# Gated experts with a four-sequence product scheme: the order of the closing pairs, and where their X and the down forms are made

## The chip, the cores and the metric

One core of a Trainium2 chip. The metric is the device time of the whole program in microseconds, the median over runs.

## The reference

A residual block of gated experts. For each of 8 sequences x[b] (512 x 256), with 8 experts and one shared expert of width 1024:

```python
g = jnp.einsum('bsd,edf->ebsf', h, Wg)
u = jnp.einsum('bsd,edf->ebsf', h, Wu)
expert_outs = jnp.einsum('ebsf,efd->ebsd', jax.nn.silu(g) * u, Wd)
expert_output = jnp.einsum('be,ebsd->bsd', gating_probs, expert_outs)
shared = jnp.einsum('bsf,fd->bsd', jax.nn.silu(h @ Sg) * (h @ Su), Sd)
return (1.0 - sg) * expert_output + sg * shared        # and x is added
```

All is float32.

## The kernel before, in words

**Units.** The work is cut into 36 units: two halves (four sequences each), nine experts (the shared one is the ninth), two groups of four 128-row blocks of the width. A unit takes four blocks of gate and up weights against four sequences, 16 products each, and builds them from fewer matmuls by sums and differences over six pairs of indices, `PAIRS`. Units are numbered from 0; units 0 to 17 are the first half, 18 to 35 the second. `u.opens` marks units 0 and 18. `closes(u)` marks the unit whose down products finish the accumulators of its half: unit 17, and unit 34, since unit 35, the last one, does its down products in another way (`tail`).

**Gate and up.** `gate_up(u, nxt)` is a generator of 52 steps ("G"): 16 steps of the hub (`Q_step`, `P_step`, `R1_step`), then six for each pair p (`R1_step`, L536, for the next pair, and `R_step`, L546). After the four `R_step` of pair p = (i, j) both `h_[i, j]` and `h_[j, i]` exist, the second one later; `finish` makes them (SiLU on ScalarE, L476, then L481 on VectorE). L541 and L551 are VectorE's work on the PSUM banks of these products. Then `h_sums` makes the tile X of the pair, the difference of the two h (L562), and notes four sums for later: rows and cols. `add_sum` does one of these sums on GpSimd (L573). A unit has 24 of them; some 14 are done while its pairs run, one at every second step, and about ten are left over for the first steps of the unit behind.

**Down.** `down(u, acc)` is a second generator ("D") for the same unit. It starts at step `TAKE` = 22 of its own unit and runs on through the first 22 steps of the unit behind. A fixed string orders both: `HUB` is "GGD" eight times, `BLOCK` is "GGDGGDGGD" for a pair. So three matmul products go by between one D step and the next. For a pair, `pair(p)` has three D steps:
- r: `Wd[p][i]` times `h_[i, j]` into a PSUM bank A that is then held (L635). It is added to the accumulator B of j (L599).
- S: `Wd[p][j]` times `h_[j, i]`. For pairs 0 to 3 (`OWN`), in most units, ScalarE first copies the accumulator S into the bank (L611), PE adds to it (L612), and ScalarE copies it back (`carried`). In a closing unit there is no copy back: the bank is subtracted from the accumulators B of i and V of p (L601). For pairs 4 and 5 the product s goes to a fresh bank (L635) with the same two subtractions.
- `Ud[p]` times X, added into A (L658). In a closing unit VectorE then adds the accumulator V to A (L662), and puts A onto the two accumulators b (L599, L601 or L603, by the factor 1/d).

There are two banks for down, po0 and po1; `new_po` takes them in turn and passes over a held one. After the pairs come the products p and q of the sums: `cols` in q (L635, or L612 in some units), `rows` in p (L612, named b), mixed with pair 5 in the order 0, 1, 2, 3, 4, p0, q0, 5, q1, p1, q2, p2, q3, p3.

**Down forms.** `make_ad` (four sums of 128x128, L407 to L411, and a doubling, L449) and `d_forms` (L456, L461) prepare the down weights of a unit on GpSimd, in its hub.

**Order.** PE and POOL run in the order in which the program is written down (`manual_schedule`); the order of VectorE and ScalarE is made by a planner. Tile `X` has two buffers, `ud` and `wd` six.

Of the kernel before, what the change touches and what calls it, by code (L numbers as in the profile page):

```python
# [12 lines left out]
ALU = mybir.AluOpType  # L13
# [4 lines left out]
def kernel(  # L18
# [38 lines left out]
    B, S, D = x.shape  # L57
    E, _, F = Wg.shape
# [5 lines left out]
    NH = B // NI  # L64
    CI = (0.0, 1.0, -1.0, 2.0)
    PAIRS = ((1, 0), (0, 2), (3, 0), (1, 2), (3, 1), (3, 2))

    OWN = (0, 1, 2, 3)

    const = ctx.enter_context(tc.tile_pool(name="const", bufs=1))  # L70
    wpool = ctx.enter_context(tc.tile_pool(name="w", bufs=5))
# [24 lines left out]
    gp = nc.gpsimd  # L96
    ve = nc.vector
# [206 lines left out]
    def first_order(u, made, *what):  # L304

        if u.n == 0:
            u.issued[what] = made
            for late, early in BEHIND.items():
                if what in (late, early) and late in u.issued and early in u.issued:
                    issue_after(u.issued[late], u.issued[early])  # L310
# [55 lines left out]
    units = []  # L366
# [84 lines left out]
    def d_forms(u, p):  # L451

        i, j = PAIRS[p]
        lo, hi = min(i, j), max(i, j)
        U = upool.tile([P, P], F32, tag="ud", name=f"ud{u.name}_{p}", bufs=6)
        gp.tensor_tensor(U, u.ad[i], u.ad[j], ALU.subtract)  # L456
        W = upool.tile([P, 2, P], F32, tag="wd", name=f"wd{u.name}_{p}", bufs=6)
        at, d = U.unsqueeze(1).to_broadcast([P, 2, P]), CI[i] - CI[j]
        for c, a in ((2.0, u.a2), (1.0, u.raw_d)):
            if d >= c:  # L460
                gp.tensor_tensor(W, at, a[:, lo : hi + 1 : hi - lo, 0:P], ALU.subtract)  # L461
                at, d = W, d - c
        u.Ud[p] = U
        u.Wd[p] = {lo: W[:, 0], hi: W[:, 1]}
# [90 lines left out]
    def h_sums(u, p):  # L555


        i, j = PAIRS[p]
        if u.n + 1 == len(units):
            return  # L560
        u.X[p] = tpool.tile([P, S], F32, tag="t", name=f"X{p}_{u.name}")
        first_order(u, ve.tensor_sub(u.X[p], u.h_[j, i], u.h_[i, j]), "X", p)  # L562
        for k, l in ((i, j), (j, i)):
            for which, n in (("rows", k), ("cols", l)):
                u.sums.append((which, n, (k, l)))
# [13 lines left out]
    def closes(u):  # L579

        return u.n + (2 if u.h + 1 == NH else 1) == len(units) * (u.h + 1) // NH

    def down(u, acc):

        def tile_of(key):
            acc[key] = apool.tile(
                [P, S], F32, tag=f"acc{key[0]}{key[1]}", name=f"acc{key[0]}{key[1]}_{u.h}"
            )
            return acc[key]

        def put(key, bank, s):

            if key not in acc:
                if s == 1.0:
                    nc.scalar.copy(tile_of(key), bank)
                else:
                    nc.scalar.mul(tile_of(key), bank, s)
            elif s == 1.0:
                ve.tensor_add(acc[key], bank, acc[key])  # L599
            elif s == -1.0:  # L600
                ve.tensor_sub(acc[key], acc[key], bank)  # L601
            else:
                ve.scalar_tensor_tensor(acc[key], bank, s, acc[key], ALU.mult, ALU.add)  # L603

        def seeded(key, w, b):

            po, k = new_po(f"{key[0]}{key[1]}_{u.name}")
            full = key in acc and not turned[k]
            turned[k] = False
            if full:  # L610
                nc.scalar.copy(po, acc[key])  # L611
            nc.tensor.matmul(  # L612
                po, w, b, start=not full, stop=True, skip_group_check=full
            )
            return po, full

        def carried(key, w, b):
            po, full = seeded(key, w, b)
            if full:
                nc.scalar.copy(acc[key], po)  # L620
            else:
                put(key, po, 1.0)
            return po if full else acc[key]

        def carried_with(key, w, b, half, s):
            po, full = seeded(key, w, b)
            assert full
            ve.scalar_tensor_tensor(
                acc[key], xhub[u.h, key[1]][:, half], s, po, ALU.mult, ALU.add
            )  # L630

        def single(key, w, b):
            po, k = new_po(f"{key[0]}{key[1]}_{u.name}")
            turned[k] = False
            nc.tensor.matmul(po, w, b, start=True, stop=True)  # L635
            return po, k

        def pair(p):
            i, j = PAIRS[p]
            d = CI[i] - CI[j]  # L640
            A, k = single(("r", p), u.Wd[p][i], u.h_[i, j])
            put(("B", j), A, 1.0)
            held[k] = True
            yield
            args = u.Wd[p][j], u.h_[j, i]
            if p in OWN and not closes(u):
                carried(("S", p), *args)
            else:
                if p in OWN:
                    o, full = seeded(("S", p), *args)  # L650
                    if not full:
                        ve.tensor_add(o, o, acc["S", p])
                else:
                    o, _ = single(("s", p), *args)
                put(("B", i), o, -1.0)
                put(("V", p), o, -1.0)
            yield
            nc.tensor.matmul(  # L658
                A, u.Ud[p], u.X[p], start=False, stop=True, skip_group_check=True
            )  # L660
            if closes(u):
                ve.tensor_add(A, A, acc["V", p])  # L662
                put(("b", i), A, 1.0 / d)
                put(("b", j), A, -1.0 / d)
            else:
                put(("V", p), A, 1.0)
            held[k] = False
            po_next[0] = 1 - k
            yield

        done = {}
        for what in (0, 1, 2, 3, 4, "p0", "q0", 5, "q1", "p1", "q2", "p2", "q3", "p3"):
            if isinstance(what, int):
                yield from pair(what)
                continue
            i = int(what[1])
            extra = carry_on.get(u.n)
            if extra is not None and extra[0] == what:
                flush_sums(u, "rows" if what[0] == "p" else "cols", i)
                if what[0] == "p":  # L680
                    key, w, b = ("b", i), u.raw_d[:, i, 0:P], u.rows[i]
                else:
                    key, w, b = ("B", i), u.ad[i], u.cols[i]
                carried_with(key, w, b, *extra[1:])
            elif what[0] == "p":
                flush_sums(u, "rows", i)
                done[what] = carried(("b", i), u.raw_d[:, i, 0:P], u.rows[i])
            else:
                flush_sums(u, "cols", i)
                po, _ = single(("q", i), u.ad[i], u.cols[i])  # L690
                put(("B", i), po, 1.0)
                done[what] = po
            if closes(u) and f"p{i}" in done and f"q{i}" in done:
                if CI[i] != 0.0:
                    put(("B", i), done[f"p{i}"], -CI[i])
                for r in (0, 1):
                    ends[u.h, i, r] = acc["bB"[r], i]
            yield
# [75 lines left out]
    def gate_up(u, nxt):  # L774
# [19 lines left out]
        for kind, i, m in hub_steps(u):  # L794
            if (kind, i, m) == ("P", 3, 0) and u.n or (kind, i, m) == ("Q", 1, 0) and u.n == 0:
                seed(u, 0)
            if (kind, i, m) == ("P", 3, 0) and u.n == 0:
                seed(u, 1)
            if kind == "Q":
                Q_step(u, i, m)  # L800
                if u.n == 0 and (i, m) == (3, 1):
                    for p, make in ahead[3:]:
                        make(u, p)
            elif kind == "P":
                P_step(u, i, m)
                if u.n == 0 and m == 1 and i in (1, 3):
                    for p, make in ahead[:2] if i == 1 else ahead[2:3]:
                        make(u, p)
            else:
                R1_step(u, 0, m)  # L810
            step += 1
            if step == 2 and u.n and nxt is not None:
                make_ad(u)
            if step in (3, 5, 7, 9, 11, 13) and u.n and nxt is not None:
                d_forms(u, (step - 3) // 2)
            yield
        if u.n == 0:
            make_ad(u)
# [58 lines left out]
                carry_on[3 + len(carry_on)] = f"{what}{i}", half, s  # L877

    TAKE = 22


    ends = {}
# [27 lines left out]
    for u in units:  # L910
# [6 lines left out]
        for what in FIRST if u.n == 0 else LAST if nxt is None else ORDER:  # L917
            if what == "G":
# [12 lines left out]
                    nc.sync.dma_start(*outgoing.pop(0))  # L931
                if nG > TAKE and nG % 2 == 0 and u.sums:
                    add_sum(u)
                for _ in range(2 if u.n and units[u.n - 1].opens else 1):
                    if nG < TAKE and u.n and units[u.n - 1].sums:
                        add_sum(units[u.n - 1])
                next(g)
# [63 lines left out]
```

## Time and profile before

| | us |
|---|---|
| median of 3 runs | 2439.89 (2439.74 to 2440.24) |
| profiled execution | 2439.38 |
| its span | 2437.6 |
| PE busy | 2427.2 |
| POOL busy | 2077.4 |
| DVE busy | 1926.9 |
| ACT busy | 1239.3 |

The span runs from the first to the last instruction of the program on the core; the execution's own time has 1.78 us around it. PE is TensorE's matmul queue, POOL is GpSimd, DVE is VectorE, ACT is ScalarE. Busy times of an engine are added without overlap. In answers by window the columns are PE, PEld (weight load), DVE, ACT, POOL with the number of instructions in brackets, then the granted TensorE clock, the DMA share and GB/s. A line of waits reads: who waited, for whom, us in total, times, longest. A product of 128x512 in float32 is two PE instructions in the profile.

### The profile page before, as it was taken

The page shows a single profiled execution, that of the slowest core. Times are in us where ns is not written, and L with a number is a line of the kernel's source. Part 1 is how long each engine was busy: PE and PEld are TensorE (multiplying, and loading weights), DVE is VectorE, ACT ScalarE, POOL GpSimd, SP SyncE. Part 2 cuts the span into 40 slices and gives each one's busy share as a digit, 9 for nine tenths or more (in the row PEclk, how much of TensorE's full clock was granted, in tenths as well). Part 3 has the DMA queues.
Part 4 walks back from the last instruction along what each step waited for, and adds up shares of the span by engine and source line. Part 5 has one row for each costly group of instructions (what it writes and reads, how often), then busy time and mean ns, then how long its engine had stood idle before and what let it go on. Part 6 is the DMA issues. An engine that isn't in the chain of part 4 may idle for free.

```text
span 2437.6 us, 22761 instructions
## 1 busy us (share of the span) xinstructions
PE 2427.2 (100%) x5736; PEld 1084.3 (44%) x5736; DVE 1926.9 (79%) x2869; ACT 1239.3 (51%) x2294; POOL 2077.4 (85%) x2313
## 2 busy tenths in 40 slices
PE   9999999999999999999999999999999999999999
PEld 4444444444444444444444444444444444444446
DVE  7778878778787877787987777777877777777795
ACT  5555554554555555555455555555455455555542
POOL 8988888898988989898888888888888888888872
PEclk9999999999999999999999999999999999999999
DMA  4333333433333332334353323322333333233245
GB/s 156 104 108 111 105 100 104 121 117 120 109 117 107 101 111 95 109 112 125 117 121 107 92 87 91 91 87 90 99 104 104 96 102 91 83 90 95 87 116 149
DMA packets 221201, 257.92 MB, mean 106 GB/s; under 512 B 64016, under 2 KB 156432, under 8 KB 221072
## 3 DMA queue, kind: packets, MB, share of 16 engines
q1 hardware_dynamic: 220240, 256.17, 35.5%
q8 instruction: 48, 0.79, 0.1%
q14 instruction: 81, 0.66, 0.1%
q10 hardware_dynamic: 832, 0.30, 0.0%
HBM read 238.59 MB, written 17.83 MB: 105 GB/s over the span
## 4 chain that ended last, share of the span: by engine, by line
PE 96%; POOL 2%; DVE 1%; ACT 0%; issue 0%; DMA 0%; DVEq 0%; POOLq 0%; ACTq 0%
PE c L546 29%; PE c L536 15%; PE c L514 10%; PE c L492 10%; PE r L635 7%; PE r L658 7%; PE S L612 5%; PE b L612 5%; PE q L635 5%; PE s L635 2%; PE tail L754 1%; POOL cols L573 0%; POOL rows L573 0%; PE B L612 0%; DVE h L481 0%; POOL wb L428 0%
## 5 line engine op out<-in xcount | busy, mean ns | idle before, releaser
L546 PE MATMUL c<-b,wb 128*128 128x512 f32 x1728 | 847.0, 592 | 0.0
L476 ACT ACTIVATE sg<-c 128x512 f32<-128x512 f32 x576 | 343.5, 597 | 585.1 <-DVE c L551 337.4
L481 DVE SCALAR_TENSOR_TENSOR h<-sg,coef,c 128x512 f32<-128x512 f32 x576 | 427.9, 743 | 237.9 <-PE c L546 138.0
L546 PEld LDWEIGHTS c<-b,wb 128*128 128x128 f32 x1728 | 328.3, 190 | 408.6 <-issue 386.2
L536 PE MATMUL c<-v,u 128*128 128x512 f32 x864 | 441.2, 593 | 0.1
L573 POOL TENSOR_TENSOR rows<-rows,h 128x512 f32<-128x512 f32 x280 | 368.8, 1317 | 0.0
L541 DVE TENSOR_TENSOR c<-D,c 128x512 f32<-128x512 f32 x432 | 298.7, 692 | 78.3 <-ACT sg L476 59.5
L573 POOL TENSOR_TENSOR cols<-cols,h 128x512 f32<-128x512 f32 x280 | 359.6, 1284 | 0.0
L551 DVE TENSOR_TENSOR c<-c,D 128x512 f32<-128x512 f32 x432 | 298.6, 691 | 20.8 <-PE c L546 20.7
L428 POOL TENSOR_TENSOR wb<-u,wb 128x256 f32<-128x256 f32 x108 | 78.5, 727 | 237.4 <-ACT wb L426 237.4
L492 PE MATMUL c<-x,w 128*128 128x512 f32 x572 | 274.5, 592 | 0.0
L536 PEld LDWEIGHTS c<-v,u 128*128 128x128 f32 x864 | 163.3, 189 | 207.4 <-issue 164.8
L635 PE MATMUL r<-h,wd 128*128 128x512 f32 x420 | 214.5, 592 | 0.0
L658 PE MATMUL r<-X,ud 128*128 128x512 f32 x420 | 214.5, 592 | 0.0
L562 DVE TENSOR_TENSOR X<-h,h 128x512 f32<-128x512 f32 x210 | 207.9, 990 | 6.8
L514 PE MATMUL c<-x,at 128*128 128x512 f32 x432 | 208.7, 593 | 0.3 <-DVE P L507 0.3
L524 ACT COPY D<-c 128x512 f32<-128x512 f32 x284 | 165.7, 584 | 80.8 <-DVE h L481 80.6
L573 POOL TENSOR_TENSOR rows<-h,h 128x512 f32<-128x512 f32 x140 | 194.6, 1390 | 0.0
L498 ACT COPY P<-c 128x512 f32<-128x512 f32 x216 | 126.5, 587 | 106.9 <-PE c L492 102.1
L573 POOL TENSOR_TENSOR cols<-h,h 128x512 f32<-128x512 f32 x140 | 180.8, 1292 | 0.0
L492 PEld LDWEIGHTS c<-x,w 128*128 128x128 f32 x572 | 108.5, 190 | 135.8 <-issue 114.1
L611 ACT COPY S<-accS 128x512 f32<-128x512 f32 x132 | 77.9, 590 | 152.1 <-DVE accV L599 140.9
(114 smaller groups left out, 3465.4 us busy)
## 6 DMA issues: line engine op xcount, KB each, us to landing
b<-xs SPq DMA_DIRECT2D x210, 512.0 KB, 3.6
v<-xs SPq DMA_DIRECT2D x210, 256.0 KB, 2.6
wd<-in_L_cond_Wd_dram SPq DMA_DIRECT2D x32, 512.0 KB, 5.0
w<-in_L_cond_Wg_dram SPq DMA_DIRECT2D x127, 128.0 KB, 3.4
w<-in_L_cond_Wu_dram SPq DMA_DIRECT2D x127, 128.0 KB, 3.5
f<-xd SPq DMA_DIRECT2D x12, 512.0 KB, 5.5
xs<-f SPq DMA_DIRECT2D x18, 256.0 KB, 2.4
xin<-in_x_dram SPq DMA_DIRECT2D x16, 256.0 KB, 4.0
```

The source lines that it names most:

```text
L476: nc.scalar.activation(s, bank, AF.Silu)
L481: made = ve.scalar_tensor_tensor(t, u.sg[i, j], coef[:, u.e, b : b + 1], bank, ALU.mult, ALU.mult)
L492: nc.tensor.matmul(bank, u.raw[i][:, m, 0], xhub[u.h, i][:, 0], start=True, stop=True)
L514: nc.tensor.matmul(bank, u.at[i][:, m], xhub[u.h, i][:, 1], start=False, stop=True, skip_group_check=True,)
L536: nc.tensor.matmul(bank, u.U[p][:, m], u.V[p], start=False, stop=True, skip_group_check=True)
L541: first_order(u, ve.tensor_sub(other, u.Ds[j, m], bank), "other", p, m)
L546: nc.tensor.matmul(bank, u.W[p][:, r, m], u.VB[p][:, r], start=False, stop=True, skip_group_check=True,)
L551: ve.tensor_add(bank, bank, u.Ds[j, m])
L573: gp.tensor_tensor(sums[n], u.h_[n, n] if first else sums[n], u.h_[at], ALU.add)
L612: nc.tensor.matmul(po, w, b, start=not full, stop=True, skip_group_check=full)
L635: nc.tensor.matmul(po, w, b, start=True, stop=True)
L658: nc.tensor.matmul(A, u.Ud[p], u.X[p], start=False, stop=True, skip_group_check=True)
```

## The change

Three things are done. In the two closing units, pairs 0 to 4 do the S product in the first of their D steps and r in the second; pair 5 keeps its order. In the same units GpSimd makes the X of pairs 1, 2, 3 and 4 in place of VectorE. In units 1, 18 and 19 (`LATE_FORMS`), `make_ad` moves from hub step 2 to step 9 and the six `d_forms` from steps 3, 5, ..., 13 to steps 10 to 15, and two left-over sums are done per step; before, two per step were done in units 1 and 19, and one in unit 18.

```diff
+    SWAPPED = 5
@@ h_sums
-        first_order(u, ve.tensor_sub(u.X[p], u.h_[j, i], u.h_[i, j]), "X", p)
+        made = (gp if closes(u) and p in (1, 2, 3, 4) else ve).tensor_tensor(
+            u.X[p], u.h_[j, i], u.h_[i, j], ALU.subtract
+        )
+        first_order(u, made, "X", p)
@@ pair(p) of down
-            A, k = single(("r", p), u.Wd[p][i], u.h_[i, j])
-            put(("B", j), A, 1.0)
-            held[k] = True
-            yield
-            args = u.Wd[p][j], u.h_[j, i]
-            if p in OWN and not closes(u):
-                carried(("S", p), *args)
-            else:
+            def first():
+                A, k = single(("r", p), u.Wd[p][i], u.h_[i, j])
+                put(("B", j), A, 1.0)
+                held[k] = True
+                return A, k
+
+            def second():
+                args = u.Wd[p][j], u.h_[j, i]
+                if p in OWN and not closes(u):
+                    carried(("S", p), *args)
+                    return
                 if p in OWN:
                     o, full = seeded(("S", p), *args)
...
                 put(("B", i), o, -1.0)
                 put(("V", p), o, -1.0)
+
+            if closes(u) and p < SWAPPED:
+                second()
+                yield
+                A, k = first()
+            else:
+                A, k = first()
+                yield
+                second()
             yield
@@ gate_up
-            if step == 2 and u.n and nxt is not None:
+            at = range(10, 16) if u.n in LATE_FORMS else range(3, 14, 2)
+            if step == at[0] - 1 and u.n and nxt is not None:
                 make_ad(u)
-            if step in (3, 5, 7, 9, 11, 13) and u.n and nxt is not None:
-                d_forms(u, (step - 3) // 2)
+            if step in at and u.n and nxt is not None:
+                d_forms(u, at.index(step))
@@
+    LATE_FORMS = (1, len(units) // NH, len(units) // NH + 1)
@@ the main loop
-                for _ in range(2 if u.n and units[u.n - 1].opens else 1):
+                for _ in range(2 if u.n in LATE_FORMS else 1):
```

## The prediction

> **What bounds the kernel now.** I read the page first: busy shares, then the chain that ended last.
>
> ```profile
> PE 2427.2 (100%) x5736; PEld 1084.3 (44%) x5736; DVE 1926.9 (79%) x2869; ACT 1239.3 (51%) x2294; POOL 2077.4 (85%) x2313
> PE 96%; POOL 2%; DVE 1%; ACT 0%; issue 0%; DMA 0%; DVEq 0%; POOLq 0%; ACTq 0%
> ```
>
> TensorE is busy all the time and carries 96% of the chain. So only what makes PE stand still can be won back, and the change removes no matmul. The waits of PE alone say how much that is:
>
> ```profile
> PE S L612 <- ACT S L611: 2.2, 4, 0.6
> PE q L635 <- POOL cols L573: 1.6, 1, 1.6
> ```
>
> Both are places that the change works on: the S products of the closing units (unit 17 near 1185 us, unit 34 near 2325 us), and one q product of unit 0's down, done in unit 1 near 90 us. The list undercounts, as a pause shorter than the tail of the matmul before it is not shown as idle. So I took the timeline of PE. A product of 128x512 is two instructions, and in undisturbed stretches products start 0.858 us apart.
>
> ```profile
> 1183.09 1.02 PE L536 MATMUL c<-v,u 128*128 128x512 f32 x2
> 1184.67 1.13 PE L612 MATMUL S<-h,wd 128*128 128x512 f32 x2 [0.55 <-ACT S L611]
> 1185.63 1.88 PE L546 MATMUL c<-b,wb 128*128 128x512 f32 x4
> ...
> 89.45 1.02 PE L514 MATMUL c<-x,at 128*128 128x512 f32 x2
> 92.05 1.13 PE L635 MATMUL q<-cols,ad 128*128 128x512 f32 x2 [1.57 <-POOL cols L573]
> 93.01 1.02 PE L536 MATMUL c<-v,u 128*128 128x512 f32 x2
> ```
>
> Around S1 (pair 1's S) the two starts lie 2.54 us apart where 1.72 would do: 0.82 lost. S2 loses 0.31 and S3 0.84 in the same way, and s4 0.16, behind the last put of pair 3. Sum 2.13 for unit 17. The windows agree: from pair 0's r to the same later product, an ordinary unit and the two closing ones:
>
> ```profile
> 1106.70:1146.18 39.48, 39.48 (x93) 17.46 (x92) 31.51 (x48) 17.71 (x34) 33.07 (x33) 1.00 0.46 137
> 1173.65:1215.27 41.62, 40.45 (x94) 17.14 (x92) 40.55 (x63) 15.56 (x29) 33.05 (x34) 1.00 0.45 137
> 2314.25:2355.87 41.62, 40.46 (x93) 17.14 (x92) 40.56 (x63) 15.58 (x29) 33.05 (x34) 1.00 0.41 124
> ```
>
> After the span come PE, PEld, DVE, ACT, POOL. Each closing window is 2.14 us longer, and there DVE is busy 40.55 of 41.62 us: in a closing unit VectorE is the bound. The granted clock is 1.00 throughout. The q product loses 93.01 - 89.45 - 1.72 = 1.84.
>
> **What the change removes.** (1) In unit 1 the POOL order was: sums, down weights (2.4 us), two sums, form 0 (1.3 us), then rows3, cols2. The q product waits for that cols2:
>
> ```profile
> 85.81 1.28 POOL L573 TENSOR_TENSOR rows<-rows,h 128x512 f32<-128x512 f32 x1
> 87.04 1.28 POOL L573 TENSOR_TENSOR cols<-cols,h 128x512 f32<-128x512 f32 x1
> 88.27 0.47 POOL L456 TENSOR_TENSOR ud<-ad,wd 128x128 f32<-128x128 f32 x1
> 88.82 0.73 POOL L461 TENSOR_TENSOR wd<-ud,wd 128x256 f32<-128x256 f32 x1
> 89.50 1.26 POOL L573 TENSOR_TENSOR rows<-rows,h 128x512 f32<-128x512 f32 x1
> 90.73 1.26 POOL L573 TENSOR_TENSOR cols<-cols,h 128x512 f32<-128x512 f32 x1
> ```
>
> With make_ad and all forms behind the ten left-over sums, cols2 ends 2.4 + 1.3 = 3.7 us earlier, at 88.3; q2's free slot is 90.31. The wait goes: **-1.84**. POOL's amount of work is the same, so u3 (L416), next in its queue, still ends near 102.0, while PE comes 1.84 earlier. Its reader starts at 108.46, now 106.6; wb for pair 2 ends 103.83, its reader moves from 109.32 to 107.5: cover 3.7 us. Late forms cost nothing while that holds; r0 reads form 0 at 102.45, now 100.6, and by then form 0 is long made (POOL is at 94.4 when it begins). No DMA is issued in the moved steps and nothing passes SP's queue; on POOL only these sums and forms change places.
>
> (2) Closing pairs. Bank: today r goes into the bank that the S before it left (free early), and S into the bank of A, the sum r + UX of the pair before, which is held until VectorE has done L662 and two puts. Then ScalarE must copy accS in (L611, 0.59), then PE goes. At S2: second put ends 1192.02, copy 1192.06 to 1192.65, PE 1192.70. With S first, S takes the early bank, copied well ahead, and r, which needs no copy, takes A's. So 0.65 us leaves the chain at the same slot.
>
> (3) X on POOL. The DVE queue from one L662 to the next, without idle time, is 1197.58 - 1189.54 = 8.04 us with an X that took 0.60 of the pitch, and 8.56 with one that took 1.13. PE needs nine products, 9 x 0.858 = 7.72. Without X both come to 7.43: DVE goes from 105-111% of PE's pace to 96%. Pairs 1 to 4 are relieved; X0 stays on DVE, but a 0.83 us gap follows it. The relief in the chain is 0.65 + 0.60 to 1.13, more than each loss (0.31 to 0.84). So the waits at S1, S2, S3 and s4 should go: **-2.13 in unit 17, -2.12 in unit 34**.
>
> What X adds to POOL: four of 1.28 each (L573, same shape, both operands in SBUF) per closing unit, 5.1 us, against POOL's idle time in 1176 to 1215:
>
> ```profile
> POOL wb L428 <- ACT wb L426: 5.1, 2, 2.8
> POOL wb L428 <- PE c L546: 3.2, 2, 1.8
> ```
>
> 8.3 us, so it fits. But X waits for the second h of its pair, and all behind it on POOL waits too: wb for pair p+2, u, at of the next unit, sums. X1 waits for h20 (ends 1181.08), so wb for pair 3 starts at 1182.4 instead of 1179.61; its reader is PE at 1189.06, 8 us after today's end. X1 is ready at 1182.4, its matmul (L658) starts at 1187.35, or 1186.5 without S1's wait. X4, behind rows0, ends near 1205.7 against 1209.6. The sums come up to 3.4 us late into unit 18, where cols2 has 1.7 us of slack before q2. That is what the second sum per step and the late forms there pay for: without make_ad and three forms ahead, cols2 ends near 1226.8 for a q2 near 1230.4. In unit 35 there are no forms, and q2's cols2 (2367.5 by the same count) has 3 us.
>
> [...] The trace: X on DVE 990 ns in the mean (1059 in this window), a POOL sum of that shape 1284 to 1317. [...]
>
> (4) The swap's own price: no row shows it. r used to be read by its put (L599) within two down slots (5.15 us) before L658 adds into the same bank; now in one, 2.57 us. L599 must end 2.5 us after r's start. Earliest end: 1.06 after PE's start (S0: 1176.22, its reader 1177.28) plus 0.69 = 1.75. With today's backlog it ended at 3.8 (r1: 1181.38, L599 to 1185.19), 3.3 (r2), 3.8 (r3), 3.2 (r4). Bounds per pair: 0 and 1.3 + 0.1 wait. Also S reads the second h, made last: h20 ends 1181.08 for a slot at 1181.38, h03 1189.63 for 1189.92, h21 1197.66 for 1197.95: always 0.29 early, as a chain of L551, L541, L481 makes it, not the backlog. Bounds: 0, or one foreign 0.6 us operation ahead of h, 0.3 + 0.1. I take 0.05 per pair, 0.5 in all, near the lower ends: with 0.28 us of DVE slack per pair, laying the 12 operations out by readiness puts L599's end at about 2.0 after r's start.
>
> Not touched: two waits of 0.34 near 1233 and 2374 (PE on a seed, L531, behind a SiLU and a copy of the same bank), and unit 0's.
>
> **Sum.** -1.84 - 2.13 - 2.12 + 0.5 = -5.6 us. The profiled execution took 2439.38, 1.78 around its span of 2437.6; the median is 0.51 above it, so 2439.89 - 5.6 = **2434.3 us**.
>
> **Rivals.**
> *Part of the waits stays* (25%). If L662 or a put lands ahead of the second h in DVE's order, S waits 0.3 + 0.1 in each of ten pairs, 4.0, and eats the closing gain of 4.25: 2439.9 - 1.84 - 0.25 = 2437.8; with half of it 2435.8. For: the margin is only 0.29. Against: in all five pairs L662 stands behind that h now.
> *The wait moves to L658* (12%). DVE's backlog stays and L599 ends 3.84 after r as in pairs 1 and 3: L658 waits 1.33 + 0.1, ten times 14.3: 2439.9 - 1.84 - 4.25 + 14.3 = 2448.1, slower; with the mean of today's four ends (3.53) 11 us, 2445. It decides from L599 2.5 us after r; break-even at 0.6 us per pair. For: DVE is at 96%, and its order is set by a planner. Against: the backlog was X.
> *The change doesn't do what it says* (3%): POOL takes X so late that L658 waits for it. That needs 4 us more lag than counted; 2440.
>
> **How the numbers follow.** 60% the forecast, within -6.1 and -4.9. About 0.2%, 4.9 us, is what a measurement of this kernel can tell from no change, so that case is just faster. Case two and the last lie within 0.2%, as does a mild form of case three (3%): 31%. Slower 9%. The range runs from -6.7 (all, and the two 0.34 waits) to case two, 2433.2 to 2438.4.
>
> **What would show it.** PE's waits without the rows for S <- ACT and q <- POOL; closing windows near 39.5, DVE busy near 36.3 there (40.55 less 4.25 of X); POOL about 5 us more per closing unit. Right in the small: L611 long before S, r directly behind the put. Wrong if PE shows r L658 <- DVE accB L599 (case three) or S <- DVE h L481 (case two), or if q2 of units 18 or 35 waits for POOL.

## The result and the profile after

The changed kernel took 2436.11 us in the median of 19 runs (lowest 2434.22, highest 2438.85). The kernel before, run 19 times beside it, took 2440.24 (2439.45 to 2443.49). The ratio of the medians is 0.998, with a 95% interval of 0.9974 to 0.9987: 4.1 us less, where 5.6 were forecast. The direction and the range held; the forecast gain was too large by 1.5 us, and 4.1 lies outside the band of 4.9 to 6.1 that had been given 60%. The profiled execution took 2435.56 us with a span of 2433.7; before it was 2439.38 with 2437.6.

The page's busy shares and the waits of PE come first.

```profile
PE 2426.4 (100%) x5736; PEld 1085.6 (45%) x5736; DVE 1919.0 (79%) x2861; ACT 1240.1 (51%) x2294; POOL 2086.1 (86%) x2321
PE S L616 <- ACT accV L599: 1.3, 1, 1.3
```

Eight instructions have moved from DVE to POOL, the eight X. PE's waits no longer hold a row for S behind its copy, nor for q behind POOL's cols. The one row for S that is left lies in unit 0, near 52 us, and does not belong to the closing units; it will turn out to matter.

The two closing windows, from pair 0's first down product to the same later product, are next.

```profile
1173.47:1213.27 39.80, 39.75 (x93) 17.39 (x93) 37.64 (x59) 15.57 (x29) 33.07 (x32) 1.00 0.48 143
2312.27:2352.07 39.80, 39.75 (x93) 17.39 (x93) 37.64 (x59) 15.57 (x29) 33.06 (x33) 1.00 0.45 131
```

Both went from 41.62 to 39.80; an ordinary unit's window is 39.48. That is 1.82 each, 3.64 together, and it is nearly the whole gain of this execution: from the start of the q2 product in unit 1 to the end of the span, before took 2345.51 us and after 2341.77, which is 3.74 less. Of the 3.82 us between the two profiled executions, only 0.08 lies ahead of q2, where the forecast had put 1.84.

Around q2, POOL's third sum of cols (cols2) and then PE now read:

```profile
86.47 1.27 POOL L577 TENSOR_TENSOR cols<-cols,h 128x512 f32<-128x512 f32 x1
91.11 1.02 PE L515 MATMUL c<-x,at 128*128 128x512 f32 x2
91.97 1.02 PE L639 MATMUL q<-cols,ad 128*128 128x512 f32 x2
92.83 1.02 PE L537 MATMUL c<-v,u 128*128 128x512 f32 x2
```

PE's starts are 0.86 apart, so q2 waits for nothing, and POOL's cols2 had ended at 87.74. Yet q2 starts at 91.97, against 92.05 before. PE came to it 1.66 us later than before (91.97 against 90.31): the wait is gone and the time is spent further ahead.

One loss is left in each closing window, at S1. Here are PE and, below it, DVE:

```profile
1180.34 1.02 PE L547 MATMUL c<-b,wb 128*128 128x512 f32 x2
1181.41 1.12 PE L616 MATMUL S<-h,wd 128*128 128x512 f32 x2
1182.37 1.02 PE L547 MATMUL c<-b,wb 128*128 128x512 f32 x2
```

```profile
1180.02 0.69 DVE L678 TENSOR_TENSOR r<-r,accV 128x512 f32<-128x512 f32 x1
1180.62 0.74 DVE L482 SCALAR_TENSOR_TENSOR h<-sg,coef,c 128x512 f32<-128x512 f32 x1
```

From L547 to S1 are 1.07 us and on to the next product 0.96, where 0.858 would do each: 0.31 lost. S1 reads the h that L482 ended at 1181.36. In this kernel DVE does L678 (L662 of before), the sum of A and V of pair 0, ahead of that h.

### The profile page after: what moved, and what is told of

The parts are those of the page before. It is cut to its first block, busy times and chain, and to the rows that moved or that the text cites. A ratio compares the mean times of both kernels' runs of the same rounds, so it can differ in the third digit from the quotient of the medians.

```text
span 2433.7 us, 22779 instructions
## 1 busy us (share of the span) xinstructions
PE 2426.4 (100%) x5736; PEld 1085.6 (45%) x5736; DVE 1919.0 (79%) x2861; ACT 1240.1 (51%) x2294; POOL 2086.1 (86%) x2321
## 4 chain that ended last, share of the span: by engine, by line
PE 97%; POOL 1%; DVE 1%; DMA 0%; issue 0%; ACT 0%; SPq 0%; ACTq 0%; DVEq 0%; POOLq 0%
PE c L547 30%; PE c L537 15%; PE c L515 10%; PE c L493 10%; PE r L639 7%; PE r L674 7%; PE b L616 5%; PE S L616 5%; PE q L639 5%; PE s L639 2%; PE tail L770 1%; PE B L616 0%; DVE h L482 0%; DMA sgt<-ondB_sharedgateprob_dram 0%; POOL wd L462 0%
## 5 line engine op out<-in xcount | busy, mean ns | idle before, releaser
L547 PE MATMUL c<-b,wb 128*128 128x512 f32 x1728 | 847.0, 592 | 0.0
L477 ACT ACTIVATE sg<-c 128x512 f32<-128x512 f32 x576 | 343.7, 597 | 570.5 <-DVE c L552 328.5
L482 DVE SCALAR_TENSOR_TENSOR h<-sg,coef,c 128x512 f32<-128x512 f32 x576 | 427.5, 742 | 243.0 <-PE c L547 133.1
L547 PEld LDWEIGHTS c<-b,wb 128*128 128x128 f32 x1728 | 328.3, 190 | 408.6 <-issue 389.1
L537 PE MATMUL c<-v,u 128*128 128x512 f32 x864 | 441.1, 593 | 0.6 <-ACT c L532 0.6
L542 DVE TENSOR_TENSOR c<-D,c 128x512 f32<-128x512 f32 x432 | 298.7, 692 | 79.3 <-ACT sg L477 60.2
L537 PEld LDWEIGHTS c<-v,u 128*128 128x128 f32 x864 | 163.4, 190 | 207.7 <-issue 166.1
L563 DVE TENSOR_TENSOR X<-h,h 128x512 f32<-128x512 f32 x202 | 196.1, 971 | 6.8
```

Of the source, the lines that this page charges most:

```text
L477: nc.scalar.activation(s, bank, AF.Silu)
L482: made = ve.scalar_tensor_tensor(t, u.sg[i, j], coef[:, u.e, b : b + 1], bank, ALU.mult, ALU.mult)
L537: nc.tensor.matmul(bank, u.U[p][:, m], u.V[p], start=False, stop=True, skip_group_check=True)
L542: first_order(u, ve.tensor_sub(other, u.Ds[j, m], bank), "other", p, m)
L547: nc.tensor.matmul(bank, u.W[p][:, r, m], u.VB[p][:, r], start=False, stop=True, skip_group_check=True,)
```

## The experiments

Each kernel is compared with the kernel before, run beside it. Given are the median of 10 or 11 runs, the lowest and the highest, and the ratio of the medians with its 95% interval. The runs of a kernel spread over 3 to 6 us, so differences of 1 us between two experiments are read from their profiles and not from the medians.

**Taking the closing units apart.** Theory: the swap and the move of X are both needed, and each alone leaves waits. Rival: one of them does it all.

```diff
 no_swap, on the changed kernel
-    SWAPPED = 5
+    SWAPPED = 0
```

> The changed kernel with r first and S second again in all pairs; GpSimd still makes X of pairs 1 to 4, forms still late. Load theory (the closing waits were VectorE being over 100% loaded by X): with 0.6 to 1.2 us of X gone per pair the last put ends early enough even with the copy of accS behind it, so no PE wait in the closing windows, 39.5 us each, and also no wait of S1 for h20 (0.32 us, twice): about 0.6 us faster than the changed kernel, 4.6 to 4.8 faster than before in the median. Bank theory (the copy L611 between put and S was the wait): PE waits for L611 stay, 0.1 to 0.6 us each at S1, S2, S3: 1 to 3 us slower than the changed kernel.

Measured: 2437.13 (2435.10 to 2440.67), ratio 0.9988 (0.9979 to 0.9997). The closing window:

```profile
1173.84:1214.24 40.40, 39.75 (x94) 17.39 (x93) 37.05 (x59) 15.49 (x29) 32.88 (x32) 1.00 0.45 141
1191.00 1.02 PE L537 MATMUL c<-v,u 128*128 128x512 f32 x2
1192.67 1.12 PE L616 MATMUL S<-h,wd 128*128 128x512 f32 x2 [0.65 <-ACT S L615]
1190.12 0.69 DVE L542 TENSOR_TENSOR c<-D,c 128x512 f32<-128x512 f32 x1 [0.51 <-ACT sg L477]
```

The first line is the window, the next two are PE at S2. With DVE relieved by X alone the losses at S1, S3 and s4 are gone. S2 still waits for its copy, 1.67 us from start to start instead of 0.86. So of the two theories written down before the run neither is right as it stands: by load no wait was to be left, by bank those at S1, S2 and S3. And the wait at S2 is not backlog. The copy stands behind the two puts, and these stood in DVE's queue behind the L542 of the last line, which was idle for ScalarE's SiLU (L477), though L678, the sum that the puts read, had ended at 1189.60.

```diff
 x_on_dve, on the changed kernel
-        made = (gp if closes(u) and p in (1, 2, 3, 4) else ve).tensor_tensor(
+        made = (gp if closes(u) and p in () else ve).tensor_tensor(
```

> The changed kernel with all X back on VectorE; swapped order and late forms stay. Load theory: VectorE needs 8.0 to 8.6 us per pair where PE needs 7.72, so 0.3 to 0.8 us per pair are still lost, only at another place (L658 behind L603 reading r, or r behind the puts): closing windows 41 to 42 us, no gain or a loss there; in all within 1 us of before, or slower. Bank theory: the copy of 0.65 us has left the chain, so windows fall by 0.65 us for each of S1, S2, S3: about 40.2 us, 2.5 to 3 us faster than before in both halves.

Measured: 2437.98 (2436.45 to 2440.19), ratio 0.9989 (0.9981 to 0.9998).

```profile
1175.37:1216.18 40.81, 40.27 (x93) 17.12 (x93) 40.08 (x63) 15.52 (x29) 34.25 (x35) 1.00 0.47 139
```

DVE is again busy nearly all of the window, 40.08 of 40.81. Three losses are left in it, counted from start to start as before: 0.32 at S1 (for its h), 0.78 at a product c (L537, which the profile puts down to POOL's wb) and 0.23 at r4 (for a put, L607). Whether the second is POOL's or follows from DVE's backlog was not tried. Here too the window lies between the two forecasts, 41 to 42 by load and about 40.2 by bank.

So X alone takes 1.22 us out of a closing window (41.62 to 40.40), the swap alone 0.81 (to 40.81), and both 1.82. Each alone leaves waits, as the theory has it, and neither part costs what the other brings.

**Unit 1.** Theory: the late forms in unit 1 take 1.84 us off. Rival: q2's wait only hid that PE is late in other executions, so that the median gains little.

```diff
 forms_unit1, on the kernel before: only unit 1's forms are late
+            at = range(10, 16) if u.n == 1 else range(3, 14, 2)
-            if step == 2 and u.n and nxt is not None:
+            if step == at[0] - 1 and u.n and nxt is not None:
                 make_ad(u)
-            if step in (3, 5, 7, 9, 11, 13) and u.n and nxt is not None:
-                d_forms(u, (step - 3) // 2)
+            if step in at and u.n and nxt is not None:
+                d_forms(u, at.index(step))
```

> The kernel before with the late forms in unit 1 alone. Cover theory (in unit 1 PE waited for the later of two chains, GpSimd's and its own out of unit 0, and its own comes 0 to 2 us late from run to run): the wait q <- cols goes in the profile, the median falls by only 0.3 to 0.9 us and the fastest runs by up to 1.8; runs spread more. Sum of the prediction: 1.84 us faster in every run.

```diff
 closing_only, on the changed kernel: unit 1's forms as before
-    LATE_FORMS = (1, len(units) // NH, len(units) // NH + 1)
+    LATE_FORMS = (len(units) // NH, len(units) // NH + 1)
...
-                for _ in range(2 if u.n in LATE_FORMS else 1):
+                for _ in range(2 if u.n == 1 or u.n in LATE_FORMS else 1):
```

> The changed kernel with the forms of unit 1 as before (units 18 and 19 keep late forms). Both theories: 2.13 + 2.12 less twice 0.32 (S1 waiting for h20) = 3.6 us faster than before. With the cover theory that is nearly the whole of the measured gain (4.1); by the sum of the prediction it would leave 1.84 to unit 1, so only 2.3 for this kernel.

Measured: forms_unit1 2440.61 (2437.77 to 2442.41), ratio 0.9998 (0.9989 to 1.0007). The wait is gone from its profile, and q2 starts without one:

```profile
90.03 1.02 PE L514 MATMUL c<-x,at 128*128 128x512 f32 x2
90.89 1.02 PE L635 MATMUL q<-cols,ad 128*128 128x512 f32 x2
```

Its fastest run is 1.56 us below the fastest of before, but its median shows no gain. closing_only took 2436.34 (2435.83 to 2438.82), ratio 0.9984 (0.9975 to 0.9993): the closing units alone give all that the whole change gives in the median, 4.0 us, with the wait of q2 still there:

```profile
89.85 1.02 PE L515 MATMUL c<-x,at 128*128 128x512 f32 x2
92.44 1.13 PE L639 MATMUL q<-cols,ad 128*128 128x512 f32 x2 [1.57 <-POOL cols L577]
```

This speaks for the rival. The medians alone do not settle it, as their intervals reach about 2 us to either side. The profiles say more. Up to q2 five of the kernels with late forms in unit 1 do the same work, and q2 starts, without a wait, at 90.89 (forms_unit1), 91.97 (after), 92.34 (no_swap), 93.87 (x_on_dve) and 94.52 (swap_not_1); with the wait it starts at 92.05 (before) and 92.44 (closing_only). So taking the wait away made PE free to come early, and it mostly did not.

It can be put in numbers. If what follows q2 takes in every run what it took in the profile, the start of q2 in a run is its time, less 1.82 us (what both profiled executions took around their spans, by these starts), less 2345.51 (before) or 2341.77 (after). By this estimate q2 starts at 92.1 in the fastest run of before and 92.9 in the median; after the change at 90.6 and 92.5. The forms take 1.5 us off the fastest run and 0.4 off the median. The profiles bear the assumption out: from the start of q2 to the end of the span are 2341.7 to 2342.0 us in the eight profiles of kernels with swap and X both changed, though q2 starts anywhere from 90.21 to 97.74 in them. The wait was a floor: a run in which PE came early was held until about 92.05, and a run in which PE came late was not held at all. The floor itself moves a little, as cols2 ended at 91.99 in the profile of before and at 92.38 in that of closing_only. The times of closing_only agree: eight of its 11 runs lie between 2435.83 and 2436.84.

**Where PE is late.** In all these kernels the order of work in unit 0 is the same, but one wait in it differs in size from profile to profile. PE's first line here is of after, and so are the two of ACT:

```profile
50.94 1.02 PE L537 MATMUL c<-v,u 128*128 128x512 f32 x2
53.24 1.12 PE L616 MATMUL S<-h,wd 128*128 128x512 f32 x2 [1.28 <-ACT accV L599]
52.09 0.63 ACT L322 ACTIVATE v<-v 128x512 f32<-128x512 f32 x1 [2.15 <-DVE v L319]
52.62 0.57 ACT L599 COPY accV<-r 128x512 f32<-128x512 f32 x1
```

S of pair 2 needs the copy accV, which frees its bank. In ACT's queue the copy stands behind the scaling of v for pair 5, and that stood idle for DVE's difference v. The S waits 0.84 us in the profile of before, 1.28 in that of after, 2.70 in no_swap, 2.16 in x_on_dve. Theory: this wait makes PE late, and moving v of pair 5 out of the copy's way brings q2 forward, in the changed kernel alone.

```diff
 v5_late_before and v5_late_after: on the kernel before, and on the changed one
-                        if u.n == 0 and p + 3 < len(PAIRS):
+                        if u.n == 0 and p + 3 < len(PAIRS) - 1:
                             x_difference(u, p + 3)
+                    if u.n == 0 and (p, m, r) == (3, 0, 1):
+                        x_difference(u, 5)
```

> The kernel before with one ScalarE operation of unit 0, the scaling of v for pair 5 (L321), issued behind the copy of A into accV (L595) and two SiLU instead of ahead of them, so that S of pair 2 in unit 0 needn't wait for it (1.0 to 2.9 us in the profiles so far). Cover theory: PE reaches q2 earlier and waits there for GpSimd's cols instead; q2 starts near 92.1 as in the fastest runs of before, so the fastest runs gain nothing (2439.3), the median at most 0.9 and the spread shrinks. If the two waits just add: 1 to 2.9 us faster in every run.

> The changed kernel with the same move of L321 in unit 0. Cover theory: with the late forms nothing hides PE's own way through unit 0, so the wait's end shows in full: median 1 to 2.5 us faster than the changed kernel (2433.6 to 2435.1), fastest runs about 0.9 faster, spread smaller. Rival (the spread of the runs comes from elsewhere than unit 0's S wait): less than 0.5 us and the same spread.

Measured: v5_late_before 2439.82 (2438.56 to 2441.52), ratio 0.9998 (0.9989 to 1.0007); v5_late_after 2435.90 (2433.61 to 2438.43), ratio 0.9981 (0.9972 to 0.999). The changed kernel's median moved by 0.2 us where the theory asked for 1 to 2.5, and the fastest run on the kernel before came 0.9 us lower (2438.56 against 2439.50), where it allowed nothing: the theory missed. The wait at S is gone in both, but a new one follows it. In v5_late_after, PE:

```profile
54.22 1.02 PE L674 MATMUL r<-X,ud 128*128 128x512 f32 x2
57.35 1.94 PE L537 MATMUL c<-v,u 128*128 128x512 f32 x2 [2.10 <-ACT c L532]
59.08 1.91 PE L547 MATMUL c<-b,wb 128*128 128x512 f32 x2
```

Now the seed of a bank (L532) is late and costs 2.10. In this profile the edit moved the wait by one pair and did not remove it. So ACT's order alone is not the cause.

```diff
 v5_dve and v5_dve_before: VectorE scales v of pair 5
-            if d != 1.0:
+            if d != 1.0 and p == 5:
+                ve.tensor_scalar(v, v, 1.0 / d, 0.0, ALU.mult, ALU.add)
+            elif d != 1.0:
                 nc.scalar.mul(v, v, 1.0 / d)
```

> The changed kernel with the scaling of pair 5's v in unit 0 done by VectorE right behind the difference (L319), no longer by ScalarE, so that no ScalarE copy or SiLU queues behind a wait for VectorE's v. If S's wait in unit 0 (1.0 to 2.9 us, and in three of ten profiles a stretch of 3.4 us at half clock behind it) makes the spread: the wait falls below 0.5 us, no half clock, median 1 to 2.5 us below the changed kernel (2433.5 to 2435), runs within 2.5 us. Rival (as with the move of L321, the wait only goes to another ScalarE or VectorE operation): median within 0.5 us of the changed kernel, same spread.

> The kernel before with the same edit as v5_dve. Cover theory: the wait of q2 for GpSimd's cols takes over what unit 0 gains: fastest runs not under 2438.5, median 0.4 to 0.9 us below before (2439.5 to 2440), while the same edit gains the changed kernel more. If the waits just add, both kernels gain the same.

```diff
 v5_pool: GpSimd scales v of pair 5, as the first step of that pair's sums
-            if d != 1.0:
+            if d != 1.0 and p != 5:
                 nc.scalar.mul(v, v, 1.0 / d)
...
+        d = CI[i] - CI[j]
...
+        if u.n == 0 and p == 5:
+            gp.tensor_scalar(v, v, 1.0 / d, 0.0, ALU.mult, ALU.add)
```

> The same, but GpSimd does the scaling, just ahead of its own use of v (0.83 us in its queue). Same expectation for S's wait; GpSimd's cols for q2 come 0.8 us later, which the late forms still cover (2 to 3 us between cols and q2 in the changed kernel's profile).

Measured: v5_dve 2435.13 (2433.58 to 2438.27), ratio 0.998 (0.9971 to 0.9989). Its profile has no wait at S and one of 0.54 at the next pair's c, and q2 starts at 90.98. On the kernel before, the same edit gave 2440.89 (2439.44 to 2442.49), ratio 1.0 (0.9991 to 1.0009), with a wait of 2.20 at that c and q2 at 92.22, right behind POOL's cols2 (92.17): the floor again. But the forecasts missed: the runs of v5_dve spread over 4.7 us and not 2.5, one us in its median is within that, and v5_dve_before was 0.35 above the kernel before, not 0.4 to 0.9 below. The same edit left 0.54 in one profile and 2.20 in the other, so it does not set the size of the wait. v5_pool missed too: 2441.55 (2439.69 to 2442.95), ratio 1.0004 (0.9995 to 1.0013). I had overlooked that PE reads v itself (L540), ahead of the sums:

```profile
53.97 1.02 PE L677 MATMUL r<-X,ud 128*128 128x512 f32 x2
60.62 2.07 PE L540 MATMUL c<-v,u 128*128 128x512 f32 x2 [5.63 <-POOL v L334]
```

It still says something: q2 starts at 97.74, 5.8 us later than in the changed kernel's profile, and the median is 5.4 us longer. Without a wait at q2, lateness from unit 0 shows in full in the time.

**The 0.31 us left at S1.** Theory: it is DVE's order, and can be undone. Rival: DVE has so little time to spare that the wait turns up elsewhere.

```diff
 swap_not_1, on the changed kernel: pair 1 keeps r ahead of S
-            if closes(u) and p < SWAPPED:
+            if closes(u) and p in (0, 2, 3, 4):
```

> The changed kernel with pair 1 of the closing units in the old order, pairs 0, 2, 3, 4 swapped. In the profile of the changed kernel the one wait left in each closing window is S1 for h20 (0.32 us with its aftermath), in that of the kernel without swap it is S2 for its copy (0.92). Here neither should be met: h20 has a slot more, and S2 finds S1's bank free early. Windows 39.5 us, 0.64 us faster than the changed kernel in span from 1000 us on; in the median inside the noise. Rival: the changed turn of the two banks brings a wait at S2 or r2, 0.3 to 0.9 us per closing unit.

```diff
 h_first, on v5_late_after: the sum of A and V of pair 0 behind h20
+                u.made = {}
...
+            u.made[i, j] = made
...
-                ve.tensor_add(A, A, acc["V", p])
+                added = ve.tensor_add(A, A, acc["V", p])
+                if p == 0:
+                    issue_after(added, u.made[PAIRS[1][::-1]])
```

> The changed kernel with L321 late in unit 0 (as in v5_late_after) and, in the closing units, the sum A + V of pair 0 (L678 in the changed kernel) ordered on VectorE behind h20 of pair 1, whose S in the changed kernel waits 0.32 us for it. If that order is the cause, S1 starts at its slot and no PE wait is left in the closing windows: 39.48 us each; from q2 of unit 1 to the end 0.6 us less than the changed kernel. Rival (something else of VectorE's queue takes the place, or r1 waits for the later puts): a wait of 0.2 to 0.4 us at r1 or L674, as with pair 1 in the old order. In the median against before 4.5 to 6 us less, by where the runs fall in unit 0.

Measured: swap_not_1 2435.97 (2434.36 to 2439.09), ratio 0.9982 (0.9973 to 0.9991); h_first 2434.08 (2433.11 to 2437.38), ratio 0.9975 (0.9966 to 0.9985). Both windows are 39.78 us, where the changed kernel has 39.80. In h_first S1 no longer waits, but r3 does, for a put (L609 there):

```profile
1173.25:1213.03 39.78, 39.75 (x94) 17.33 (x93) 37.46 (x59) 15.49 (x29) 32.99 (x32) 1.00 0.48 144
1198.14 1.02 PE L539 MATMUL c<-v,u 128*128 128x512 f32 x2
1199.19 1.12 PE L641 MATMUL r<-h,wd 128*128 128x512 f32 x2
1197.25 0.70 DVE L544 TENSOR_TENSOR c<-D,c 128x512 f32<-128x512 f32 x1 [0.65 <-ACT sg L478]
1197.85 1.28 DVE L609 SCALAR_TENSOR_TENSOR accb<-r,accb 128x512 f32<-128x512 f32 x2
```

1.05 us lie between PE's two starts, and swap_not_1 has the same between c and r3 (1200.91 and 1201.97). As the rival has it, the wait goes from one operation to another, and 0.3 us per closing unit stay. But its reason is not what DVE shows: DVE stood idle for 0.65 us, in both kernels, behind ScalarE's SiLU, with the put queued behind that L544, though the sum that the put reads (L680) had ended at 1196.60. What is left is again an order of DVE's queue; whether another order would end it was not tried.

The last kernel puts v5_late and swap_not_1 together:

> Both: L321 late in unit 0 and pair 1 not swapped. If both hold, 1.6 to 3 us faster than the changed kernel, median 2433 to 2434.5.

Measured: 2434.05 (2433.60 to 2437.30), ratio 0.9976 (0.9967 to 0.9985). It and h_first have the lowest medians, 6.3 us below before. But up to the first closing unit both run the same program as v5_late_after, and behind it they differ from that by 0.04 us in two windows; their other 1.8 us are where the runs happened to fall in unit 0. Their intervals overlap that of the changed kernel, so it is not shown that they beat it.

## Why the prediction was right or wrong

**Step 1, unit 1: the mis-sized term.** The mechanism was right: cols2 ended at 87.74 (88.3 was forecast) and the wait went. The term "-1.84" was wrong as a change of the time. It took q2's free slot, 90.31, from one execution and treated it as fixed. PE was there at 90.31 in that execution, but at 91.97, 92.34, 93.87 and 94.52 in the profiles of after, no_swap, x_on_dve and swap_not_1, and then there is little or nothing to win. By the estimate above the term is -1.5 in the fastest runs and -0.4 between the medians. With -0.4 in place of -1.84 the prediction's own sum gives 4.15 us, and 4.1 were measured; this agreement is no separate proof, since the -0.4 is itself what the medians leave beside the 3.74 us behind q2. What speaks for it separately is forms_unit1, with no gain in the median, and closing_only, with 4.0.

**Steps 2 and 3, the closing units: right in the sum.** Forecast were -4.25 for the waits and +0.5 for the swap, -3.75; both windows together gave -3.64. The experiments show both parts: without X DVE's backlog and with it three of the four losses are gone, and the swap takes ScalarE's copy off the path. The copy mattered less than argued: once X was away it cost PE time at S2 alone, and there through DVE's order. The moved X came where they were counted. Here is POOL in the first closing unit:

```profile
1181.43 1.28 POOL L563 TENSOR_TENSOR X<-h,h 128x512 f32<-128x512 f32 x1 [4.78 <-DVE h L482]
1185.27 0.75 POOL L417 TENSOR_TENSOR u<-at,at 128x256 f32<-128x256 f32 x1
1192.79 0.73 POOL L410 TENSOR_TENSOR at<-w 128x256 f32<-128x256 f32 x1
1204.40 1.27 POOL L563 TENSOR_TENSOR X<-h,h 128x512 f32<-128x512 f32 x1 [0.70 <-DVE h L482]
```

X1 ended at 1182.71 and X4 at 1205.67 (forecast 1182.4 and 1205.7), and cols2 of unit 18 at 1226.22 (1226.8). An X took 1.27 to 1.28, as the row of a sum had said. That is 1.2 times VectorE's mean in this stage of the kernel before (1.059); but against the 0.68 of an X on VectorE that nothing held up (last section) it is 1.9 times. So the means of 990 and 1059 ns in the prediction are those of a VectorE that GpSimd holds up. No product waited for an X (the third rival).

**DVE's 36.3 us: wrong, without effect.** It stayed busy 37.64 us per window. The four X took 4.1 us of instruction time along, but back to back an instruction's last 0.09 us lie under the next one's start (the L678 at 1180.02 in the changed kernel is 0.69 long, and the next starts 0.60 after it), and where the queue has gaps they do not. The sum of instruction times fell by 4.1, the busy time by 2.91.

**Step 4, the price of the swap: near by luck.** It was taken as 0.5 and came out as 0.64, twice 39.80 - 39.48. But the place differs: not 0.05 in each pair, but about 0.31 at one, which is the mechanism of the first rival, *part of the waits stays* (L662 ahead of the second h), in one pair of five. The argument against it, that L662 stood behind that h in all five pairs, used the old order, and the swap changed that order. Here is DVE at the same place, first no_swap, then x_on_dve:

```profile
1180.53 0.74 DVE L482 SCALAR_TENSOR_TENSOR h<-sg,coef,c 128x512 f32<-128x512 f32 x1
1181.19 0.69 DVE L678 TENSOR_TENSOR r<-r,accV 128x512 f32<-128x512 f32 x1
```

```profile
1181.92 0.69 DVE L678 TENSOR_TENSOR r<-r,accV 128x512 f32<-128x512 f32 x1
1182.52 0.74 DVE L482 SCALAR_TENSOR_TENSOR h<-sg,coef,c 128x512 f32<-128x512 f32 x1
```

With X moved and no swap, h20 comes first, as of old; with the swap and X on DVE, L678 does. The second rival, the wait at L658, did not occur: the put behind r ended 1.75 us after r's start in pair 1 (1185.84 after 1184.09) and at most 1.92 after it in the others, where 2.0 was forecast and 2.5 was the limit.

**What stays open.** Why v of pair 5 comes at another time in every execution was not tested; no experiment moved the work ahead of it. The kept profiles point to the way in which VectorE and GpSimd hold each other up, which the last section shows. Here are that v and the X just ahead of it on DVE in unit 0, first in before, then in no_swap:

```profile
48.01 0.99 DVE L562 TENSOR_TENSOR X<-h,h 128x512 f32<-128x512 f32 x1
48.92 1.21 DVE L318 TENSOR_TENSOR v<-x,x 128x512 f32<-128x512 f32 x1
```

```profile
49.03 1.67 DVE L563 TENSOR_TENSOR X<-h,h 128x512 f32<-128x512 f32 x1
50.62 1.75 DVE L319 TENSOR_TENSOR v<-x,x 128x512 f32<-128x512 f32 x1
```

Where they took 0.99 and 1.21 (five profiles of 14, to 0.01), PE's wait in unit 0 was 0.84 to 0.90 at S, or 0.30 and 0.54 at the next c in the kernels with pair 5 edited. Where they took 1.67 and 1.75 (eight profiles), it was 2.16 to 2.71 and 1.85 to 2.20, leaving v5_pool aside. The profile of after, with 0.98 and 1.75, lies between with 1.28. best and v5_late_after do the same work in unit 0 and had 0.30 and 2.10. So the two engines' turns, more than the edits, seem to set the wait.

## What to carry to other kernels

A wait in one profiled execution is the later of two arrivals, and only the difference between them can be won: before it is counted, look at the earlier arrival in several executions, or compare the fastest run with the median. A wait early in a program can be a floor that hides the spread of what lies ahead of it, and then taking it away lowers the fastest runs more than the median. In the closing units, where VectorE was busy for 40.55 of 41.62 us, taking work away from it was what shortened the stage most, and two reorderings only moved the last short wait. But before load is blamed for such a wait, look at whether the engine stood idle just ahead of it: here it did, with the work that was needed queued behind.

## What was not expected of the hardware

**VectorE and GpSimd stood in each other's way by turns.** In the kernel before, the first closing unit, an X of two SBUF operands on DVE and POOL's sums:

```profile
1181.60 1.20 DVE L562 TENSOR_TENSOR X<-h,h 128x512 f32<-128x512 f32 x1
1190.14 0.68 DVE L562 TENSOR_TENSOR X<-h,h 128x512 f32<-128x512 f32 x1
```

```profile
1180.98 1.27 POOL L573 TENSOR_TENSOR rows<-h,h 128x512 f32<-128x512 f32 x1
1182.20 1.18 POOL L416 TENSOR_TENSOR u<-at,at 128x256 f32<-128x256 f32 x1
1190.18 1.23 POOL L409 TENSOR_TENSOR at<-w 128x256 f32<-128x256 f32 x1
```

The first X began inside POOL's rows, took 1.20, and ended 0.55 after it; the u that POOL began inside this X took 1.18 and ended 0.58 after the X. The second X began 0.04 ahead of POOL's at, took 0.68, and the at took 1.23. The timelines of both engines show the same through the whole kernel before. Of the 210 X on DVE, the 149 that began with 0.2 us or more of a POOL instruction still to run ended 0.54 to 0.56 us after that instruction, and so took 0.78 to 1.76 us; the other 61 took 0.68 to 0.70. Of POOL's sums of 128x256, the 129 that began inside an X, more than 0.15 us ahead of its end, took 1.06 to 1.24 us and ended 0.58 to 0.60 after it; of the other 908, all but 8 took 0.71 to 0.74. In both counts the one that began later ended 0.54 to 0.60 us behind the other. With X on POOL the u and the at took 0.75 and 0.73, 0.43 and 0.50 less. This is part of why POOL's busy time grew by less than the eight X, 10.2 us by their durations: from 2077.4 to 2086.1 over the whole program.

**A clock stage came in some executions and not in others.** Behind the long wait in unit 0 PE ran at half its rate for a while in the profiles of x_on_dve, v5_late_after and swap_not_1, after recorded waits of 2.16, 2.10 and 2.71 us: in the second, products started 1.73 and 1.71 us apart, twice the usual 0.858. The granted clock was 0.79 over the 8 us from 53 to 61 us in all three; at half the rate that makes an estimate of 0.21 x 8 / 0.5 = 3.4 us for the stage. The first three products behind the wait took 4.29, 4.35 and 4.20 us from start to start, where they took 2.68 in the profile of after: it cost 1.5 to 1.7 us each time. In no_swap the same wait, as long as in swap_not_1, had no such stage. First swap_not_1, then no_swap, each with PE at the end of the wait and the window from 53 to 61 us:

```profile
54.27 2.08 PE L616 MATMUL S<-h,wd 128*128 128x512 f32 x2 [2.71 <-ACT accV L599]
53.00:61.00 8.00, 6.73 (x12) 3.03 (x13) 5.09 (x9) 3.17 (x6) 8.00 (x8) 0.79 0.47 149
```

```profile
53.61 1.12 PE L616 MATMUL S<-h,wd 128*128 128x512 f32 x2 [2.70 <-ACT accV L599]
53.00:61.00 8.00, 7.39 (x17) 3.34 (x18) 6.57 (x10) 4.37 (x11) 8.00 (x8) 1.00 0.57 185
```

The granted clock is 0.79 in the one window and 1.00 in the other. It is 1.00 there in v5_late_before too, behind a wait of 2.11. So of these five waits of 2.10 to 2.71 us three were followed by the stage and these two were not, and the length did not tell which; what does is not shown here.

The stage also shows in the times. The mean granted clock of the runs is on record too. Four profiled executions have 0.999: the three above and v5_pool, where the first product behind the wait of 5.63 took 2.07 us, as in x_on_dve and swap_not_1 (2.07 and 2.08; 1.12 in after and no_swap). Ten have 1.000, and in five of them (before, after, no_swap, v5_late_before, best) the clock was 1.00 in every window from 45 to 80 us. Of the 19 runs of the changed kernel the seven with 0.999 lie between 2437.21 and 2438.85, the twelve with 1.000 between 2434.22 and 2436.51. If the runs at 0.999 had the stage, as these profiled executions did, much of the spread, and of PE's lateness at q2, goes with it. It goes into the medians as well: v5_late_after had four runs at 0.999 of eleven, best and h_first one of ten each. Sorted in this way, which was done afterwards and on few runs, unit 1's late forms are worth 0.8 us (forms_unit1 against before) and 1.2 (after against closing_only, not run side by side) in the medians of the runs at 1.000, and 0.5 and 0.0 in those at 0.999, as a floor would have it.
